# The second layer of a two-layer convolution kernel written as a fixed pipeline over half images

## The chip, the cores and the metric

The kernel runs on one core of one Trainium2 chip. The metric is the device time of one execution, in microseconds (us); lower is better. The core has five engines with instruction queues of their own: TensorE (PE, with its weight loads shown apart as PEld), VectorE (DVE), ScalarE (ACT), GpSimd (POOL) and SyncE (SP). Transfers between DRAM and on-chip memory are issued from the SP and ACT queues and carried out by 16 DMA engines.

## The reference

The input `x` is 32 images of 8 channels and 256 x 256 pixels, float32. Layer 0 normalises it in groups, runs 15 steps of a coupled map lattice beside a small neural convolution, and mixes the two through a gate; the result is added to `x`. Layer 1, the one that the change touches, normalises again, quantises, convolves 3 x 3 over 8 channels and adds its input:

```
def _L1_conv_ref(x, weight, bias):
    sx = 127.0 / jnp.max(jnp.abs(x));  sw = 127.0 / jnp.max(jnp.abs(weight))
    qx = clip(round(x * sx), -127, 127);  qw = clip(round(weight * sw), -127, 127)
    out = conv3x3(qx, qw) / (sx * sw)          # 'same' padding
    return out + bias[None, :, None, None]
x = x + _L0_conv_ref(_gn(x), ...)              # layer 0
x = x + _L1_conv_ref(_gn(x), weight, bias)     # layer 1
```

The scale `sx` needs the largest normalised value of all 32 images, so layer 1 can't start before layer 0 has finished.

## The kernel before

The kernel has two stages. The first (lines 257 to 895) computes layer 0 in groups of four images and leaves each image's result in a DRAM scratch tensor `y_s[b]`. The second stage (lines 898 to 963) reads those tensors and does layer 1; the change is confined to it.

An image lies in the second stage as a tile of 128 partitions by 19 bands by 256 columns. A partition is one of 16 rows times 8 channels, and a band is a set of 16 rows of which 14 are outputs, so that neighbouring bands overlap by two rows. The steps for image `b` are:

- Line 909, `load`: one DMA of 2432 KB brings `y_s[b]` into a `yb` buffer, of which there are four. Images 0 to 2 are loaded from the SP queue, the rest from the ACT queue.
- Line 940: three VectorE instructions subtract the mean and scale, one for the first band, one for bands 1 to 17 (4352 columns) and one for the last band, because the edge bands mask rows. The result is the float32 tile `tq`, of which there is one.
- Line 944: one VectorE instruction over all 4864 columns adds and subtracts 1.5 x 2^23, which rounds to an integer.
- Line 946: one VectorE instruction clips to -127..127 and writes bf16 into `qt`, whose rows are 258 columns long with a zero at either end. There are two `qt`.
- Line 953: for each of ten pairs of bands (the last is a single band) three matmuls of 512 columns add up the three horizontal taps in a PSUM tile, of which there are four. Line 954: ScalarE scales it, adds the bias and writes it to the output tile `ob` (two of them).
- Line 957: one VectorE instruction over 4864 columns adds the image itself, `ob = ob + yb`.
- Line 960: 19 DMAs on the SP queue, one for each band, store the 14 output rows of the 8 channels (112 KB each, the last 32 KB).

In this stage the order of the instructions is a scheduler's: the code gives an order by image, and a planner interleaves images as it expects things to be ready. On VectorE it often lets two line-957 additions or two images' lines 940 to 946 follow each other. On the ACT queue it puts the loads in pairs, after every second image's ten line-954 instructions.

The transfers of all queues share eight completion counters, handed out in turn in the planned order of issue. A transfer waits, on the queue that issues it, until the transfer that had its counter before has landed. In the built program of before nearly every store of line 960 carries such a wait, and when the transfer eight places earlier is an image load, the store waits for the whole load.

Of the kernel before, what the change touches and what calls it, by code (L numbers as in the profile page):

```python
# [31 lines left out]
F32 = mybir.dt.float32  # L32
BF16 = mybir.dt.bfloat16
F32R = mybir.dt.float32r
AF = mybir.ActivationFunctionType
ALU = mybir.AluOpType
AX = mybir.AxisListType
DRAM = bass.MemoryType.DRAM
PSUM = bass.MemoryType.PSUM

P = 128
C = 8
# [4 lines left out]
MAX_Q = 127.0  # L47
ROUND = 1.5 * 2.0**23

NB = 19  # L50
STEP = 14
PW = W + 2
# [61 lines left out]
def kernel(  # L114
# [15 lines left out]
    nc = tc.nc  # L130
    B = x.shape[0]
    V, S, G, T = nc.vector, nc.scalar, nc.gpsimd, nc.tensor

    def dram_ap(t, offset, dims):
        return bass.AP(t.tensor, t.offset + offset, dims)
# [17 lines left out]
    qw = cp.tile([P, 3, P], BF16, name="qw")  # L153
# [6 lines left out]
    mean_y = cp.tile([P, B], F32, name="mean_y")  # L160
# [96 lines left out]
    with ExitStack() as one:  # L257

        one.enter_context(tc.manual_schedule(engines={mybir.EngineType.PE}))
        pool = lambda name, bufs, **kw: one.enter_context(tc.tile_pool(name=name, bufs=bufs, **kw))  # L260
# [115 lines left out]
        def lattice(g):  # L376
# [77 lines left out]
            if g == 0:  # L454
                units[0], dmas = load(0)
                for d in dmas:
                    nc.sync.dma_start(*d)
                for ts in tiles:
                    begin(units[0], ts)
            for c in range(C):  # L460
                u = g * C + c
                ds = units[u]
                for step in range(STEPS):
                    if step == 7 and u + 1 < NG * C:
                        units[u + 1], dmas = load(u + 1)
                        later.extend(dmas)
# [363 lines left out]
        def chain(*gens):  # L830
            for gen in gens:
                yield from gen
# [15 lines left out]
        def both(a, t_a, b, t_b):  # L848

            done_a = done_b = 0.0  # L850
            while a or b:
                if b is None or a and done_a * t_b <= done_b * t_a:
                    w = next(a, None)
                    if w is None:
                        a = None
                        continue
                    done_a += w
                else:
                    w = next(b, None)
                    if w is None:  # L860
                        b = None
                        continue
                    done_b += w
                yield w

        def prep(g, halves):
            return normalise([(b, half) for half in halves for b in range(g * GB, g * GB + GB)])

        def images(f, g):
            for b in range(g * GB, g * GB + GB):  # L870
                yield from f(b)
# [3 lines left out]
        def after(g, gen):  # L875

            while issued[0] < stored[g]:
                yield 4.0
            yield from gen
# [3 lines left out]
        for g in range(NG):  # L883
            fill, t = images(nca, g), T_NCA
            if g:
                fill, t = both(fill, t, after(g - 1, images(gate, g - 1)), T_GATE), t + T_GATE
            if g + 1 < NG:
                fill, t = both(fill, t, prep(g + 1, (0, 1)), T_PREP), t + T_PREP
            if g == 0:
                fill, t = chain(prep(0, (1,)), fill), t + 20.0  # L890
# [7 lines left out]
    with ExitStack() as two:  # L898


        pool = lambda name, bufs, **kw: two.enter_context(
            tc.tile_pool(name=name, bufs=bufs, reuse_waits="tile", **kw)
        )
        tp, qp, op, sp, yp = pool("tp", 1), pool("qp", 2), pool("op", 2), pool("sp", 1), pool("yp", 4)
        ps = pool("ps", 4, space=PSUM)

        def load(b):
            y = yp.tile([P, NB, W], F32, name="yb", tag="yb")
            (nc.sync if b < 3 else nc.scalar).dma_start(
                y, dram_ap(y_s[b], 0, [[W, P], [STEP * C * W, NB], [1, W]])  # L910
            )
            return y

        ys = {b: load(b) for b in range(3)}

        gmax = sp.tile([P, 1], F32, name="gmax")
        V.tensor_reduce(gmax, dev_y, AX.X, ALU.max)
        gall = sp.tile([P, 1], F32, name="gall")
        G.partition_all_reduce(gall, gmax, P, bass.bass_isa.ReduceOp.max)
        sx = sp.tile([P, 1], F32, name="sx")  # L920
        V.reciprocal(sx, gall)
        V.tensor_scalar(sx, sx, MAX_Q, None, ALU.mult)
        inv = sp.tile([P, 1], F32, name="inv")
        V.tensor_tensor(inv, sx, sw, ALU.mult)
        V.reciprocal(inv, inv)
        qs = sp.tile([P, 3, B], F32, name="qs")
        V.tensor_scalar(qs[:, 0, :], rstd_y, sx, None, ALU.mult)
        V.tensor_scalar(qs[:, 1, :], qs[:, 0, :], masks[:, 2:3], None, ALU.mult)
        V.tensor_scalar(qs[:, 2, :], qs[:, 0, :], masks[:, 3:4], None, ALU.mult)
        qt = [qp.tile([P, NB, PW], BF16, name=f"qt{i}", tag=f"qt{i}", bufs=1) for i in range(2)]  # L930
        for t in qt:
            V.memset(t[:, :, 0], 0.0)
            V.memset(t[:, :, PW - 1], 0.0)

        for b in range(B):
            y = ys.pop(b)

            t = tp.tile([P, NB, W], F32, name="tq", tag="tq")
            for k0, k1, i in ((0, 1, 1), (1, NB - 1, 0), (NB - 1, NB, 2)):
                V.tensor_scalar(  # L940
                    t[:, k0:k1, :], y[:, k0:k1, :], mean_y[:, b : b + 1], qs[:, i, b : b + 1],
                    ALU.subtract, ALU.mult,
                )
            V.tensor_scalar(t, t, ROUND, ROUND, ALU.add, ALU.subtract)
            q = qt[b % 2]
            V.tensor_scalar(q[:, :, 1 : 1 + W], t, MAX_Q, -MAX_Q, ALU.min, ALU.max)
            o = op.tile([P, NB, W], F32, name="ob", tag="ob")
            for p in range(10):
                k0, n = 2 * p, (2 if p < 9 else 1)
                pt = ps.tile([P, 512], F32, name="pt2", tag="pt2")  # L950
                pt = pt[:, : n * W].rearrange("p (k w) -> p k w", w=W)
                for dx in range(3):
                    T.matmul(pt, qw[:, dx, :], q[:, k0 : k0 + n, dx : dx + W], start=(dx == 0), stop=(dx == 2))  # L953
                S.activation(o[:, k0 : k0 + n, :], pt, AF.Identity, bias=bv[:, 3:4], scale=inv)  # L954
            if b + 3 < B:
                ys[b + 3] = load(b + 3)
            V.tensor_tensor(o, o, y, ALU.add)
            for k in range(NB):
                rows = STEP if k < NB - 1 else 4
                nc.sync.dma_start(  # L960
                    dram_ap(out, b * C * H * W + STEP * k * W, [[W, rows], [H * W, C], [1, W]]),
                    o[C : C + rows * C, k, :],
                )


# [43 lines left out]
```

## Time and profile before

| | us |
|---|---|
| median of the runs shown (three, 14333.49 to 14348.35) | 14336.46 |
| the profiled execution's own time | 14416.5 |
| its span in the profile | 14414.7 |
| first line-940 instruction of the second stage | 13652.1 |
| second stage from there to the end of the span | 762.6 |
| second stage per image | 23.8 |

| engine | busy over the span |
|---|---|
| PE | 13267.4 us (92%) |
| DVE | 8213.1 us (57%) |
| ACT | 4039.8 us (28%) |
| POOL | 2445.9 us (17%) |

The page puts each engine's busy time beside the span, but these shares are averages over two very different stages. PE is busy at 90% or more in nearly every slice up to the first stage's end; in the last slices it falls to a third. The second stage is read by asking the trace for that stretch alone: the groups of instructions in it, what each engine's and the SP queue's waits ended on, and the chain of work that ended last. "SPq" and "ACTq" are the instruction queues as issuers of DMAs.

### The profile page before, as it was taken

Reading aid. Unit: us, or ns where it says so; the run is one execution under the profiler, and the core shown is the slowest. Engines: PE = TensorE matmul, PEld = TensorE weight load, DVE = VectorE, ACT = ScalarE, POOL = GpSimd, SP = SyncE. Lnnn points to the kernel's source line nnn. Section 1 sums busy time; section 2 is a strip of 40 time slices with the busy share of each in tenths; the row PEclk is TensorE's granted clock in tenths of the full one; section 3 lists DMA queues with packets and bytes.
Section 4 is the critical chain, followed back from the end, with each engine's and each line's share of the span. In section 5 each row is a group of like instructions: output and inputs, shape, how many; then the busy total and the mean of one; then the engine's idle time right before and its main releaser. Section 6 shows DMA issues by size and latency. Waiting matters only on the chain.

```text
span 14414.7 us, 229163 instructions
## 1 busy us (share of the span) xinstructions
PE 13267.4 (92%) x81728; PEld 6423.3 (45%) x81728; DVE 8213.1 (57%) x16290; ACT 4039.8 (28%) x6274; POOL 2445.9 (17%) x4266
## 2 busy tenths in 40 slices
PE   2999999999999999999999999999999999999833
PEld 1554444444444444444444444444444444444311
DVE  3555555555555555555555555555555555555576
ACT  1333232232222222222322223222323222222122
POOL 1111111111111111111111111111111111112300
PEclk9999999999999999999999999999999999999966
DMA  5444444444444444444444434444444433333465
GB/s 148 93 97 92 90 103 106 103 94 100 110 94 100 99 106 94 103 100 95 100 103 107 98 93 106 110 94 94 104 104 98 103 88 88 80 83 78 122 195 176
DMA packets 2259559, 1496.74 MB, mean 104 GB/s; under 512 B 1061248, under 2 KB 2229504, under 8 KB 2258304
## 3 DMA queue, kind: packets, MB, share of 16 engines
q1 hardware_dynamic: 2176976, 1401.95, 41.9%
q10 hardware_dynamic: 81456, 80.12, 1.7%
q8 instruction: 664, 10.88, 0.3%
q14 instruction: 463, 3.79, 0.1%
HBM read 866.48 MB, written 478.69 MB: 93 GB/s over the span
## 4 chain that ended last, share of the span: by engine, by line
PE 70%; DMA 9%; DVE 9%; SPq 5%; issue 3%; POOL 2%; ACT 1%; ACTq 1%; POOLq 0%; DVEq 0%
PE pt L487 31%; PE ph L567 18%; PE pa L759 13%; PE acc L584 7%; DVE gt L495 2%; DMA im<-xp_s 1%; PE pg L725 1%; DMA xp_s<-lo 1%; SPq L545 1%; DVE m_b L500 1%; DMA xb<-in_x_dram 1%; DMA m_a<-m_a 1%; DMA out_dram<-ob 1%; SPq L960 1%; PE pt L953 1%
## 5 line engine op out<-in xcount | busy, mean ns | idle before, releaser
L487 PE MATMUL pt<-m_a,lw 128*64 128x390 f32 x17280 | 5827.0, 497 | 186.4 <-DMA m_a<-m_a 122.4
L487 PE MATMUL pt<-m_b,lw 128*64 128x384 f32 x17280 | 5796.6, 492 | 19.2 <-DVE m_b L410 18.0
L577 ACT ACTIVATE h<-ph,bp_sb 128x512 f32<-128x512 f32 x4096 | 2584.6, 684 | 6491.5 <-PE ph L567 6423.0
L487 PEld LDWEIGHTS pt<-m_a,lw 128*64 128x64 f32 x17280 | 2298.4, 138 | 1884.0 <-issue 1681.2
L487 PEld LDWEIGHTS pt<-m_b,lw 128*64 128x64 f32 x17280 | 2306.6, 138 | 1560.0 <-issue 1423.6
L567 PE MATMUL ph<-im,wp_hi 48*128 48x512 f32 x12288 | 2800.2, 419 | 174.2 <-DVE gt L495 113.1
L567 PE MATMUL ph<-im,wp_lo 48*128 48x512 f32 x12288 | 2675.2, 402 | 0.0
L495 DVE SCALAR_TENSOR_TENSOR gt<-pt,d_b 128x390 f32<-128x390 f32 x2880 | 1605.3, 557 | 1714.7 <-PE pt L487 1711.2
L495 DVE SCALAR_TENSOR_TENSOR gt<-pt,d_a 128x384 f32<-128x384 f32 x2880 | 1580.3, 549 | 1694.5 <-PE pt L487 1694.1
L504 POOL TENSOR_TENSOR m_b<-m_b,junk 128x12 f32<-128x12 f32 x2688 | 795.5, 296 | 8193.8 <-DVE m_b L500 7517.2
L567 PEld LDWEIGHTS ph<-im,wp_hi 48*128 48x128 f32 x12288 | 1417.5, 189 | 1081.7 <-DVE gt L495 303.9
L500 DVE SCALAR_TENSOR_TENSOR m_b<-gt 128x390 f32<-128x390 f32 x2688 | 1546.1, 575 | 44.5 <-DVE gt L495 2.3
L500 DVE SCALAR_TENSOR_TENSOR m_a<-gt 128x384 f32<-128x384 f32 x2688 | 1522.3, 566 | 17.2
L567 PEld LDWEIGHTS ph<-im,wp_lo 48*128 48x128 f32 x12288 | 1417.0, 189 | 217.3
L584 PE MATMUL acc<-h,wu_z 128*32 128x512 f32 x8320 | 1165.6, 603 | 6.1 <-ACT nca L602 5.5
L759 PE MATMUL pa<-xnb,gw 128*64 128x512 f32 (+1 forms) x3840 | 879.9, 588 | 43.7 <-DVE xnb L700 43.5
L759 PE MATMUL pa<-cmb,gw 128*64 128x512 f32 (+1 forms) x3840 | 857.6, 577 | 17.4 <-POOL cmb L681 17.4
L759 PE MATMUL pa<-nb,gw 128*64 128x512 f32 (+1 forms) x3840 | 863.6, 576 | 0.0
L730 POOL TENSOR_TENSOR d<-cmb,nb 128x512 f32<-128x512 f32 x320 | 502.9, 1572 | 1460.6 <-DVE gate L734 1028.5
L700 DVE TENSOR_SCALAR xnb<-xb,sc 128x256 f32<-128x256 f32 x608 | 290.7, 493 | 796.7 <-DMA xb<-in_x_dram 759.5
L953 PE MATMUL pt<-qt,qw 128*128 128x512 bf16 (+1 forms) x960 | 269.5, 451 | 477.0 <-ACT ob L954 425.4
L734 DVE TENSOR_TENSOR gate<-gate,d 128x512 f32<-128x512 f32 x320 | 217.4, 679 | 764.7 <-ACT gate L727 756.7
(132 smaller groups left out, 6928.0 us busy)
## 6 DMA issues: line engine op xcount, KB each, us to landing
im<-xp_s SPq DMA_DIRECT2D x1152, 193.5 KB
im<-xp_s SPq DMA_DIRECT2D x1216, 96.8 KB
d_a<-xq_s SPq DMA_DIRECT2D x2048, 36.0 KB
nb<-nc_s SPq DMA_DIRECT2D x288, 256.0 KB
cq<-cm_s SPq DMA_DIRECT2D x288, 256.0 KB
yb<-y_s ACTq DMA_DIRECT2D x29, 2432.0 KB
xb<-in_x_dram SPq DMA_DIRECT2D x544, 128.0 KB
xp_s<-hi SPq DMA_DIRECT2D x256, 258.0 KB
```

The lines of the kernel that those rows point to most:

```text
L487: T.matmul(pt[half], lw[:, c, k, half], beside if part == 2 else own, start=part < 2, stop=part > 0,)
L495: V.scalar_tensor_tensor(gt, pt, FLOOR, d[:, ts, :], ALU.max, ALU.add)
L500: V.scalar_tensor_tensor(to, gt, 1.0, gt, ALU.subtract, ALU.mult)
L504: G.tensor_tensor(edge, edge, junk.unsqueeze(1).to_broadcast([P, 6, 2]), ALU.mult)
L567: T.matmul(ph[:, :n].rearrange("p (h w) -> p h w", w=W), w[64 * i : 64 * i + 48, dx, :], rhs[:, :, dx : dx + W], start=(dx == 0 and w is w ...
L577: S.activation(h[:, :n], ph[:, :n], AF.Relu, bias=bp_sb)
L584: T.matmul(acc[32 * g : 32 * g + 32, :cols], wu_z[:, 24 - 8 * i : 56 - 8 * i], h, start=first, stop=last,)
L700: V.tensor_scalar(xnb[:, k, 1 : 1 + W], xb[:, k, :], sc[:, i : i + 1], sc[:, 1:2], ALU.subtract, ALU.mult,)
L730: G.tensor_tensor(three(d), cmb[:, :n, 1 : 1 + W], nin, ALU.subtract)
L734: V.tensor_tensor(y[:, :cols], gt[:, :cols], d[:, :cols], ALU.mult)
L759: T.matmul(three[half], gw[:, s * 3 + dx, half], t[:, :n, dx : dx + W], start=(i == 0), stop=(i == 8),)
L953: T.matmul(pt, qw[:, dx, :], q[:, k0 : k0 + n, dx : dx + W], start=(dx == 0), stop=(dx == 2))
```

## The change

Only the second stage changes.

- Its instructions now stand on every engine in the order in which the code gives them; no scheduler moves them.
- An image is worked on in two halves, of bands 0 to 9 and 10 to 18. `tq` and `ob` become half-image tiles (two and four of them), `qt` becomes two half tiles for each of two images, and there are eight PSUM tiles. The 3 x 3 taps need no other half's data, since bands overlap.
- Rounding and clipping are arranged anew on VectorE. One instruction adds the rounding constant and takes the maximum with the constant minus 127; a second takes the minimum with the constant plus 127, subtracts the constant and writes bf16.
- In each iteration VectorE first scales and quantises both halves of image `b`, then adds both halves of image `b - 1`. SP stores bands 0 to 12 of image `b - 1`. ScalarE evacuates image `b`, then its queue stores bands 13 to 18 of image `b - 1` and issues the load of image `b + 3`.
- The first four images are loaded from SP. The zero columns of `qt` are set by GpSimd, not VectorE.

In the order of the built program the counters of the stores and loads are handed out, from the fifth image on, so: store 1 of SP for image j, store 1 of ACT for image j - 1, and so on in turn up to the sixth of each; then store 7 of SP, the load that stands behind the ACT stores of image j - 1, and stores 8 to 13 of SP. That makes 20 transfers an image, and each waits for the one eight places before it in that list. ACT's first store of an image so waits for the load of the iteration before, and ACT's fourth for SP's store 13 of the same image.

```diff
+        two.enter_context(tc.manual_schedule())
...
-        tp, qp, op, sp, yp = pool("tp", 1), pool("qp", 2), pool("op", 2), pool("sp", 1), pool("yp", 4)
-        ps = pool("ps", 4, space=PSUM)
+        tp, qp, op, sp, yp = pool("tp", 2), pool("qp", 1), pool("op", 4), pool("sp", 1), pool("yp", 4)
+        ps = pool("ps", 8, space=PSUM)
...
-            (nc.sync if b < 3 else nc.scalar).dma_start(
+            (nc.sync if b < 4 else nc.scalar).dma_start(
...
-            V.tensor_scalar(t, t, ROUND, ROUND, ALU.add, ALU.subtract)
-            q = qt[b % 2]
-            V.tensor_scalar(q[:, :, 1 : 1 + W], t, MAX_Q, -MAX_Q, ALU.min, ALU.max)
...
+        HALVES = ((0, 10), (10, NB))
+        def scaled(b, y, h):
+            h0, h1 = HALVES[h]
+            t = tp.tile([P, 10, W], F32, name="tq", tag="tq")
             for k0, k1, i in ((0, 1, 1), (1, NB - 1, 0), (NB - 1, NB, 2)):
+                k0, k1 = max(k0, h0), min(k1, h1)
+                if k0 < k1:
+                    V.tensor_scalar(
+                        t[:, k0 - h0 : k1 - h0, :], y[:, k0:k1, :], mean_y[:, b : b + 1],
+                        qs[:, i, b : b + 1], ALU.subtract, ALU.mult,
+                    )
+            t = t[:, : h1 - h0, :]
+            V.tensor_scalar(t, t, ROUND, ROUND - MAX_Q, ALU.add, ALU.max)
+            return t
+        def quantised(b, t, h):
+            V.tensor_scalar(qt[b % 2][h][:, :, 1 : 1 + W], t, ROUND + MAX_Q, ROUND, ALU.min, ALU.subtract)
...
+        last = None
+        for b in range(B + 1):
+            if b < B:
+                y = ys[b]
+                ts = [scaled(b, y, h) for h in range(2)]
+                for h in range(2):
+                    quantised(b, ts[h], h)
+            if last:
+                i, os_ = last
+                yi = ys.pop(i)
+                for h, (h0, h1) in enumerate(HALVES):
+                    o = os_[h][:, : h1 - h0, :]
+                    V.tensor_tensor(o, o, yi[:, h0:h1, :], ALU.add)
+                store(nc.sync, i, os_[0], 0, range(0, 10))
+                store(nc.sync, i, os_[1], 1, range(10, 13))
+            done = last
+            if b < B:
+                last = b, [convolved(b, h) for h in range(2)]
+            if done:
+                i, os_ = done
+                store(nc.scalar, i, os_[1], 1, range(13, NB))
+                if i + 4 < B:
+                    ys[i + 4] = load(i + 4)
```

`convolved(b, h)` holds the matmuls and the ScalarE instruction of before for the bands of one half, and `store` the DMA of before for the bands that it is given.

More of the change, by code (lines that the diff above doesn't have):

```diff
@@ L912, in load @@
             return y
-        ys = {b: load(b) for b in range(3)}
+        ys = {b: load(b) for b in range(4)}
         gmax = sp.tile([P, 1], F32, name="gmax")
@@ L929, with convolved @@
         V.tensor_scalar(qs[:, 2, :], qs[:, 0, :], masks[:, 3:4], None, ALU.mult)
[L930 to L938, printed above, removed]
-            for k0, k1, i in ((0, 1, 1), (1, NB - 1, 0), (NB - 1, NB, 2)):
[L940 to L944, printed above, removed]
-            q = qt[b % 2]
[L946 to L949, printed above, removed]
+        qt = [[qp.tile([P, n, PW], BF16, name=f"qt{i}{j}") for j, n in enumerate((10, 9))] for i in range(2)]
+        for t in (*qt[0], *qt[1]):
+            G.memset(t[:, :, 0], 0.0)
+            G.memset(t[:, :, PW - 1], 0.0)
+        HALVES = ((0, 10), (10, NB))
+        def scaled(b, y, h):
+            h0, h1 = HALVES[h]
+            t = tp.tile([P, 10, W], F32, name="tq", tag="tq")
+            for k0, k1, i in ((0, 1, 1), (1, NB - 1, 0), (NB - 1, NB, 2)):
+                k0, k1 = max(k0, h0), min(k1, h1)
[9 more added lines that the diff above has]
+            V.tensor_scalar(qt[b % 2][h][:, :, 1 : 1 + W], t, ROUND + MAX_Q, ROUND, ALU.min, ALU.subtract)
+        def convolved(b, h):
+            h0, h1 = HALVES[h]
+            o = op.tile([P, 10, W], F32, name="ob", tag="ob")
+            for k0 in range(0, h1 - h0, 2):
+                n = min(2, h1 - h0 - k0)
                 pt = ps.tile([P, 512], F32, name="pt2", tag="pt2")
@@ L952, with store @@
                 for dx in range(3):
-                    T.matmul(pt, qw[:, dx, :], q[:, k0 : k0 + n, dx : dx + W], start=(dx == 0), stop=(dx == 2))
+                    T.matmul(
+                        pt, qw[:, dx, :], qt[b % 2][h][:, k0 : k0 + n, dx : dx + W],
+                        start=(dx == 0), stop=(dx == 2),
+                    )
                 S.activation(o[:, k0 : k0 + n, :], pt, AF.Identity, bias=bv[:, 3:4], scale=inv)
[L955 to L958, printed above, removed]
+            return o
+        def store(queue, b, o, h, ks):
+            for k in ks:
                 rows = STEP if k < NB - 1 else 4
-                nc.sync.dma_start(
+                queue.dma_start(
                     dram_ap(out, b * C * H * W + STEP * k * W, [[W, rows], [H * W, C], [1, W]]),
-                    o[C : C + rows * C, k, :],
+                    o[C : C + rows * C, k - HALVES[h][0], :],
                 )
+        last = None
[21 more added lines that the diff above has]
+                    ys[i + 4] = load(i + 4)
 def kernel(
```

## The prediction

> **What bounds the kernel now.** The first stage keeps its instructions and their order on every engine, so only the second stage counts. I asked for the busy time of the engines in stretches of it (columns: stretch, length, busy time and count of each engine, PE clock, DMA share, GB/s).
>
> ```profile
> 13650.00:13666.00 16.00, 2.69 (x7) 0.99 (x7) 14.78 (x14) 0.78 (x1) 0.38 (x1) 0.50 1.10 348
> 14000.00:14100.00 100.00, 35.83 (x130) 14.58 (x129) 69.37 (x25) 27.90 (x42) 0.00 (x0) 0.66 0.62 190
> ```
>
> The first row is the loading of the first images, the second the steady state. There no engine is full: DVE 69%, PE 36%, ACT 28%, DMA 62%. Next, the groups of instructions from 13660 on, shapes apart:
>
> ```profile
> L954 ACT ACTIVATE ob<-pt,bv,inv 128x512 f32<-128x512 f32 x288 | 204.3, 777 | 536.7 <-DMA out_dram<-ob 456.9 <-PE pt L953 52.4 <-DMA yb<-y_s 22.8
> L946 DVE TENSOR_SCALAR qt<-tq 128x4864 bf16<-128x4864 f32 x32 | 167.1, 5221 | 122.7 <-PE pt L953 121.0
> L957 DVE TENSOR_TENSOR ob<-ob,yb 128x4864 f32<-128x4864 f32 x32 | 167.1, 5221 | 96.0 <-ACT ob L954 77.1 <-DMA out_dram<-ob 18.9
> L944 DVE TENSOR_SCALAR tq<-tq 128x4864 f32<-128x4864 f32 x31 | 83.5, 2694 | 1.1
> L940 DVE TENSOR_SCALAR tq<-yb,mean_y,qs 128x4352 f32<-128x4352 f32 x31 | 78.8, 2541 | 0.0
> L940 DVE TENSOR_SCALAR tq<-yb,mean_y,qs 128x256 f32<-128x256 f32 x62 | 25.3, 408 | 0.7
> ```
>
> ScalarE stood 457 us for stores to release `ob`; VectorE's own waits follow from that (through PE and ACT). So the stores: their issue times, what SP waited for, and the chain of one pair of images.
>
> ```profile
> L960 SPq DMA_DIRECT2D out_dram<-ob x608: 652/817/1345, 13682.5 to 14411.6; - x152
> L909 ACTq DMA_DIRECT2D yb<-y_s x29: 366/366/395, 13637.5 to 14315.2; - x29
> ```
> ```profile
> SPq L960 <- DMA yb<-y_s: 125.8, 26, 12.0
> SPq L960 <- DVE ob L957: 49.0, 12, 4.6
> ```
> ```profile
> 14013.93 10.31 DMA yb<-y_s
> 14024.24 0.02 issue
> 14024.25 0.83 SPq L960
> ...
> 14028.75 6.96 DMA out_dram<-ob
> 14035.71 0.02 issue
> ...
> 14035.77 4.37 DMA out_dram<-ob
> 14040.15 0.78 ACT ob L954
> ```
>
> Stores stand on SP every 0.89 us (14024.25, then 14026.04 and 14027.82, each two further). 608 x 0.89 = 541 us, plus about 190 us of waits, fills the 732 us from the first store to the end. The largest wait, 126 us, is a store whose counter was last held by an image load. The bound is the SP queue: 19 stores (16.9 us) and some 6 us of waits make the 23.8 us an image.
>
> **What the Trainium skill says.** "DMA: Bandwidth & Descriptors", section "Issuing engines are not separate DMA queues": transfers from all issuers share the same 16 DMA engines, and a second issuer saves only sequencer time. Here that time is the bound (0.89 us a store at 62% DMA share), so the trace agrees there is something to save. "VectorE: DVE Perf Modes", section "What auto-detection actually checks": an instruction with one source runs two columns a cycle if source and destination are in on-chip memory with outermost dimensions both even or equal. The trace agrees: line 944 takes 0.55 ns a column, line 946, whose destination is 19 rows at a pitch of 258, takes 1.07, and this line, whose destination is rows at a pitch of 258 in even number, 0.67 with its fixed part:
>
> ```profile
> L342 DVE CAST hi<-xr 128x1024 fp32r<-128x1024 f32 x128 | 88.4, 690 | 264.8 <-DMA xp_s<-hi 195.2 <-DMA im<-xp_s 34.0 <-issue 22.3
> ```
>
> **The change, part by part, for one image.**
>
> *VectorE.* Lines 940's two shapes give 0.521 ns a column plus 0.275 us. Scaling: two edge bands 0.82, 2304 columns 1.48, 2048 columns 1.34, sum 3.63. Rounding with the lower clip, in place as line 944 (0.521 ns plus 0.16): 2560 and 2304 columns, 1.49 + 1.36 = 2.85. Upper clip into `qt`: ten rows are even, so I take 1.49; nine rows against a flat source of 2304 stay at one column a cycle, 2304 x 1.042 + 0.15 = 2.55; sum 4.04 (bounds: 2.85 if both are fast, 5.37 if neither). Addition at line 957's rate: 2.82 + 2.55 = 5.37. Total 15.9, with ten gaps of some 0.03 us 16.2; before it was 16.5. So VectorE gains next to nothing, and 32 x 16.2 is its floor.
>
> *PE and ACT.* Work is unchanged: 279.3 / 32 = 8.7 and 222.4 / 32 = 6.95 us. Eight PSUM tiles let PE run eight pairs ahead of ScalarE. VectorE adds an image one iteration after quantising it, so ACT may be late by about 12 us before VectorE stands.
>
> *SP.* 13 x 0.89 = 11.5 us instead of 16.9. *ACT queue.* 6.95 + 6 stores + one load of 0.37. No store of this shape was issued from ACT before. The nearest rows (load 0.366 there against 0.386 on SP) say the queues cost the same, so 0.89, 5.3 us in all; bounds 0.31 (the first stage's small zero stores on ACT) and 1.8 (both queues served by one generator).
>
> *DMA.* 4.59 MB an image. Loads alone ran at 348 GB/s, mixtures at up to 386: 12 to 13 us an image, not the bound.
>
> *The new wait.* ACT's first store waits until the load issued one iteration earlier has landed. Behind it on ACT's queue are five stores, the next load, and then the ten evacuations of the next image, for which PSUM, the additions and SP's stores wait. So loads form a ring: landing time L, then six stores (5.3), then the next load. L: the load at 14013.93 took 10.31 us with some 4.5 stores beside it (the bytes moved up to 14026 less its own 2.49 MB); the one at 13682.54 took 12.23 with about 10. So L = 8.8 + 0.34 k. With SP storing every 0.89 us, about six of its 13 stores fall into the six-store stretch of ACT, k is 7 to 9 and L 11.2 to 11.9. Ring: 11.6 + 5.4 = 17.0, and I allow 0.2 for a counter not yet free: 17.2 us an image. That is above VectorE's 16.2, so the ring binds. Other waits on counters (ACT's fourth store on SP's 13th; SP's ninth on ACT's fourth) close rings of 13 us or less and hide under it.
>
> *Start.* VectorE starts at 13652.1 as before, held by the reduction over partitions. The eight small sets on GpSimd end before the first matmul. Iteration 0 takes 10.7, iteration 1 starts at 13662.8. Load 4 leaves after SP's first 13 stores, at 13690; loads 5, 6 and 7 follow at spacings of 17 to 20 us, since here the counters go round in another order, and load 7 goes at about 13746.
>
> *Sum.* Load 31 is 24 rounds later: 13746 + 24 x 17.2 = 14159, landing at 14170.5. Then image 31 is scaled and quantised (10.7), image 30's first half added (2.8), and from there SP has 26 stores (23.1) and a landing of 2.9: 39.5 us. End 14210, against 14414.7: a gain of 205 us. The profiled execution (14416.5) is 80 us above the median of the runs shown; the second stage being a twentieth of it, I take the gain as it is: 14336.5 - 205 = **14131**.
>
> **Rivals.**
>
> *VectorE binds.* If ACT's stores are cheaper, or fewer SP stores meet the loads, the ring falls below 16.2. Image 31 starts at 13662.8 + 30 x 16.2 = 14149; with 39.5 the end is 14188, or 14110 as a time (14085 if both upper clips are fast). Against it: the ring is longer by the numbers above. If neither half clips fast, VectorE needs 17.5, and the time is 14150.
>
> *The two queues pay for each other.* Their stores may share what takes the 0.82 us. Six stores of ACT then take about 10 us, the ring is 21.8 us, the end 110 us later: 14245; half of it gives 14190. For it: one shared set of DMA engines, and stores that landed in 2.1 us alone took 6.96 beside a load. Against it: SP went on storing at its cadence when ACT issued a load.
>
> *Slower.* The same ring, at the price of 25.7 us a round: the point from which the gain is gone, since 205 / 24 = 8.5 more. With L = 12 each of ACT's stores would have to hold its queue for 2.3 us. Against it: the longest issue of a store on SP was 1.345. If it is 3 us, the ring is 30 us and the time 14435.
>
> *The change doesn't do what it says*: the half of nine rows keeps the old clip rate, so the new clip is fast in one half only. That is in the sum already.
>
> **Chances.** Ring at about 17.2: 0.5, its own range 14105 to 14160. VectorE binds: 0.2. Queues pay for each other: 0.22. A ring near or above 24 us: 0.08, of which 0.05 end as a loss, 0.02 within 0.2% and 0.01 as a small gain. Range 14080 to 14215: it leaves out the dearer half of the third case and the last. A measurement of this kernel can tell about 0.2% (29 us) from no change. Faster 0.93, same 0.02, slower 0.05.
>
> **What the new profile would show.** Stores on SP and ACT at 0.8 us each; second stage near 558 us; PE as before. The ring is right if ACT's first store of each image waits for `yb`, at one load each 17 us. If VectorE binds, its share is above 95% and its idle time nil. If queues pay for each other, issue times rise above 1.2 us. The clip into ten rows should take 1.5 us, into nine 2.55. The prediction fails if the landing of loads grows with both queues storing, or if the wait for the counter is placed differently from the built order.

## The result and the profile after

| | before | after |
|---|---|---|
| median of four runs each, us | 14337.08 (14333.49 to 14348.35) | 14132.78 (14127.72 to 14143.41) |
| ratio to before, 95% interval | | 0.9857 (0.984 to 0.9874) |
| the profiled execution's own time, us | 14416.5 | 14143.41 |
| its span, us | 14414.7 | 14141.6 |
| first scaling instruction of the second stage | 13652.1 | 13591.7 |
| second stage from there to the end of the span | 762.6 | 549.9 |

The change saves 204 us by the medians. The spans differ by more, 273 us, because the profiled execution of before was 60 us longer in the first stage, whose instructions are the same in both. The second stage alone is 213 us shorter, from 23.8 to 17.2 us an image, and that is the figure to work with.

The busy time of a stretch in the steady state of the kernel after (columns as in the prediction: stretch, length, PE, PEld, DVE, ACT, POOL, PE clock, DMA share, GB/s):

```profile
13800.00:13900.00 100.00, 51.57 (x180) 21.06 (x180) 90.92 (x60) 39.57 (x60) 0.00 (x0) 0.70 0.86 274
```

VectorE has gone from 69% to 91% and the DMA engines from 0.62 to 0.86. Neither is full. The groups of instructions of the kernel after from 13600 on, shapes apart, say what the rest of VectorE's time is:

```profile
L967 ACT ACTIVATE ob<-pt,bv,inv 128x512 f32<-128x512 f32 x288 | 197.0, 792 | 340.2 <-DMA out_dram<-ob 292.6 <-PE pt L963 34.1 <-DVE tq L944 13.5
L992 DVE TENSOR_TENSOR ob<-ob,yb 128x2560 f32<-128x2560 f32 x32 | 90.1, 2816 | 1.7 <-ACT ob L967 1.7
L953 DVE TENSOR_SCALAR qt<-tq 128x2304 bf16<-128x2304 f32 x32 | 81.6, 2549 | 0.0
L953 DVE TENSOR_SCALAR qt<-tq 128x2560 bf16<-128x2560 f32 x31 | 46.2, 1489 | 0.0
L944 DVE TENSOR_SCALAR tq<-yb,mean_y,qs 128x256 f32<-128x256 f32 x62 | 25.4, 409 | 40.2 <-DMA yb<-y_s 40.2
```

VectorE's only stop worth a name is the last row's: 40 us, before the first band of an image, for the image's load. Before the change it stood 121 us for PE at line 946 and 96 us at line 957. The clip (line 953) takes 1.49 us into ten rows and 2.55 us into nine. ScalarE still shows 293 us of idle time, but VectorE no longer waits for ScalarE (1.7 us), so that idle time costs nothing now.

Which of them sets the pace is read from the chain of work that ended last, here one round of the steady state up to the load that begins the next (columns: start, us, what):

```profile
13853.42 11.35 DMA yb<-y_s
...
13864.85 0.83 ACTq L973
...
13868.40 0.82 ACTq L973
...
13869.32 0.68 ACTq L973
13870.00 0.04 issue
13870.04 11.40 DMA yb<-y_s
```

Between the two loads lie six stores of the ACT queue (line 973), and nothing else is in the chain: a load lands, the store that waits for its counter goes, five more follow it, the next load goes. Such a closed chain, each round of which must end before the next can begin, is called a ring here. The rounds next to this one take 16.6 to 17.3 us. The issues of the kernel after, by line and queue (columns: count, shortest, median and longest ns, first and last start):

```profile
L973 SPq DMA_DIRECT2D out_dram<-ob x416: 807/813/1282, 13614.7 to 14138.2; - x139
L973 ACTq DMA_DIRECT2D out_dram<-ob x192: 666/823/1243, 13617.1 to 14133.4; - x192
L910 ACTq DMA_DIRECT2D yb<-y_s x28: 373/460/466, 13623.8 to 14091.2; - x28
```

A store costs the same on both queues, 0.81 and 0.82 us. Load 7 went at 13679.50 and load 31, the last, at 14091.2: 24 rounds of 17.15 us, in which a load took 11.2 to 13.1 us to land, 11.8 on average. And SP's own waits for a load have nearly gone, from 126 us in 26 waits to:

```profile
SPq L973 <- DMA yb<-y_s: 13.0, 3, 6.6
```

### The profile page after: what moved, and what is told of

The parts are those of the page before. It is cut to its first block, busy times and chain, and to the rows that moved or that the text cites. A ratio compares the mean times of both kernels' runs of the same rounds, so it can differ in the third digit from the quotient of the medians.

```text
span 14141.6 us, 229388 instructions
## 1 busy us (share of the span) xinstructions
PE 13255.7 (94%) x81728; PEld 6412.2 (45%) x81728; DVE 8184.6 (58%) x16414; ACT 4036.5 (29%) x6274; POOL 2452.2 (17%) x4274
## 4 chain that ended last, share of the span: by engine, by line
PE 73%; DMA 9%; DVE 8%; SPq 4%; issue 3%; ACTq 1%; POOL 1%; ACT 1%; POOLq 0%; DVEq 0%
PE pt L487 32%; PE ph L567 19%; PE pa L759 14%; PE acc L584 7%; DVE gt L495 2%; DMA yb<-y_s 2%; PE pg L725 1%; DMA im<-xp_s 1%; SPq L545 1%; DMA xp_s<-lo 1%; DVE m_b L500 1%; DMA xb<-in_x_dram 1%; DMA m_a<-m_a 1%; ACTq L973 1%; SPq L444 1%
## 5 line engine op out<-in xcount | busy, mean ns | idle before, releaser
L500 DVE SCALAR_TENSOR_TENSOR m_a<-gt 128x384 f32<-128x384 f32 x2688 | 1528.2, 569 | 17.2
L759 PE MATMUL pa<-cmb,gw 128*64 128x512 f32 (+1 forms) x3840 | 858.5, 577 | 17.3 <-POOL cmb L681 17.3
L700 DVE TENSOR_SCALAR xnb<-xb,sc 128x256 f32<-128x256 f32 x608 | 292.0, 495 | 762.6 <-DMA xb<-in_x_dram 725.9
L771 ACT ACTIVATE r<-pa,bv 128x512 f32<-128x512 f32 x320 | 213.0, 666 | 1538.6 <-PE pa L759 1538.5
```

Source lines behind the costliest of these rows:

```text
L500: V.scalar_tensor_tensor(to, gt, 1.0, gt, ALU.subtract, ALU.mult)
L700: V.tensor_scalar(xnb[:, k, 1 : 1 + W], xb[:, k, :], sc[:, i : i + 1], sc[:, 1:2], ALU.subtract, ALU.mult,)
L759: T.matmul(three[half], gw[:, s * 3 + dx, half], t[:, :n, dx : dx + W], start=(i == 0), stop=(i == 8),)
L771: S.activation(r1[:, : n * W], pa[:, : n * W], AF.Relu, bias=bv[:, 0:1])
```

## The experiments

When the experiments ran, the kernel before took 14382 to 14386 us (medians of seven to nine runs), some 45 us more than above. So each run is compared by its ratio to the runs of before beside it, and by the length of its second stage in its trace, which is 549.9 us for the kernel after. The kernel after itself was run once more there:

> The changed kernel itself, for comparison on one chip with the two below. All theories: a ratio of 0.986 to the kernel before, second stage 550.

It took 14162.8 us, 219 us less than before there, ratio 0.9849 (0.9835 to 0.9862), second stage 551.6 us. The two kernels whose stage was measured twice differ by 1.7 and 1.4 us in it, so stage lengths, each from one trace, can be compared to about 2 us. Mean rounds below are taken from load 7 to load 31, as above.

| run | second stage, us | time, us | ratio to before, 95% interval |
|---|---|---|---|
| kernel after, again | 551.6 | 14162.8 | 0.9849 (0.9835 to 0.9862) |
| nine-row clip fast | 554.8 | 14186.09 | 0.9858 (0.9842 to 0.9875) |
| loads from GpSimd | 534.0 | 14151.32 | 0.9839 (0.9825 to 0.9854) |
| both of these | 537.1 | 14145.14 | 0.9828 (0.9813 to 0.9842) |
| four stores on ACT | 581.9 | 14200.34 | 0.9871 (0.9856 to 0.9886) |
| nine stores on ACT | 530.9 | 14156.99 | 0.9839 (0.9824 to 0.9853) |
| the same, again | 532.3 | 14145.08 | 0.9839 (0.9826 to 0.9852) |
| nine stores on ACT, nine-row clip fast | 529.8 | 14158.58 | 0.9841 (0.9828 to 0.9855) |
| load ahead of ACT's stores | 630.1 | 14247.59 | 0.9906 (0.9891 to 0.9921) |
| all stores on SP | 618.8 | 14241.86 | 0.9898 (0.9882 to 0.9915) |
| kernel before, six stores on ACT | 704.7 | 14321.34 | 0.9951 (0.9936 to 0.9966) |

The theory is that the ring of loads and ACT stores binds. The first rival is that VectorE does.

**Is it VectorE?** The nine-row half's `tq` gets rows of 258 columns, so that its clip reads and writes rows of one pitch.

```diff
-            t = tp.tile([P, 10, W], F32, name="tq", tag="tq")
+            t = tp.tile([P, 10, W + 2 * h], F32, name="tq", tag=f"tq{h}", bufs=1)[:, :, :W]
```

> The changed kernel, with the second half's tq tile at a row pitch of 258, so that the upper clip reads nine rows and writes nine rows. Its 2.55 us should fall to about 1.36, so VectorE has about 1.2 us less to do for each image; nothing else changes. Ring theory: VectorE only waits longer for loads, period 17.15 as before, second stage 548 to 550, time about 14132. VectorE theory: 32 x 1.2 = 38 us less, about 14095.

The nine-row clip fell from 2.55 to 1.49 us, which leaves VectorE some 0.9 us an image less work (the rounding, now on the same padded rows, rose from 1.36 to 1.49). The second stage took 554.8 us, no less than before the edit (the 3 to 5 us more are about what its loads took longer to land, 11.94 us on average against 11.77). What VectorE saved it waits: its stops at line 992 rose from 2 to 18 us, and its waits for the load, in the kernel with the fast nine-row clip, rose from 40.2 us in 24 waits to

```profile
DVE tq L944 <- DMA yb<-y_s: 55.6, 26, 3.7
```

and its busy time in the steady state fell:

```profile
13934.90:14034.90 100.00, 50.05 (x180) 20.85 (x179) 84.21 (x58) 38.37 (x59) 0.00 (x0) 0.70 0.84 270
```

An engine with less work and the same end isn't the bound. This rival falls.

**Cutting the ring.** If the ring binds, a load that doesn't stand behind ACT's stores should free it. Loads 4 to 31 go out from GpSimd, whose transfers don't take part in the counters of the other two queues in the built program; in the trace of this kernel no store waits for a load.

```diff
-            (nc.sync if b < 4 else nc.scalar).dma_start(
+            (nc.sync if b < 4 else nc.gpsimd).dma_start(
```

> The changed kernel, with loads 4 to 31 issued from GpSimd's queue instead of ACT's. They then use completion counters of their own, and no store waits for a load. Ring theory (load landing plus six ACT stores sets 17.15 us an image): the ring is cut, VectorE's 15.3 us an image binds, second stage 550 - 24 x 1.85 = about 505 us, time about 14090. VectorE theory (the 17.15 us are VectorE's work and the gaps between its instructions): no change, 550 us and 14133. DMA theory (the 16 DMA engines at a share of 0.86 are what limits): no change either, or slower if loads from GpSimd's queue are made less efficiently.

The second stage fell to 534.0 us: the ring was the bound, since cutting it moved the end and relieving VectorE didn't. But the gain was 16 to 18 us instead of 45. A stretch of this kernel says what bound next:

```profile
13807.10:13907.10 100.00, 56.06 (x186) 21.25 (x185) 96.68 (x62) 39.67 (x60) 13.44 (x6) 0.73 0.84 275
```

VectorE is at 97%, so it now binds, but in most rounds with a period of 15.97 us (the loads at 13808.69 and 13824.66), where its instructions need 15.3: so far apart start images 1 to 3 in the kernel after, before the ring holds them. The groups of the same kernel show the difference in one place:

```profile
L949 DVE TENSOR_SCALAR tq<-tq 128x2560 f32<-128x2560 f32 x32 | 67.5, 2110 | 1.1
L949 DVE TENSOR_SCALAR tq<-tq 128x2304 f32<-128x2304 f32 x32 | 43.5, 1360 | 1.1
```

The rounding of the ten-row half takes 2.11 us on average instead of 1.49, that of the nine-row half the 1.36 that it took before. The timeline of one image:

```profile
13808.69 2.24 POOL L910 DMA_DIRECT2D yb<-y_s  x1 [13.73 <-DVE ob L992]
13810.02 2.20 DVE L949 TENSOR_SCALAR tq<-tq 128x2560 f32<-128x2560 f32 x1
```

GpSimd takes 2.24 us to issue a load, released by the addition that frees the image buffer, and so always at the same place in VectorE's order. The slowed instruction is the one that overlaps the end of the issue. The first two and the last two images, which no load of GpSimd meets, show 1.49 us. The Trainium skill, "SBUF — State Buffer", section "Who interferes with whom", names a cause that my 505 us left out: VectorE, when it takes two columns a cycle, and GpSimd, which needs the same port to write a transfer's descriptors, lock each other out for a whole instruction. This trace agrees as far as it goes: line 944's 2304 columns, already running when the issue begins, keep their 1.47 us, and the next instruction pays; it ends 1.29 us after the issue, a little less than its own 1.49. 28 slowed instructions at 2.20 and four at 1.49 make the 67.5 us of the row. So 0.71 us of each image, 20 of the missing 29 us, are this collision. Another 7 us are stops of VectorE at line 992, where ScalarE was late because stores had not yet freed `ob`.

With both edits together VectorE is relieved as well:

> Loads from GpSimd's queue and the fast clip in both halves together. In the run with loads from GpSimd's queue VectorE was the bound (16.0 us an image, 0.6 of it one rounding instruction made slower while GpSimd issued a load). If VectorE still binds, the period falls by 1.2 to about 14.8, second stage about 495. If stores and their counters bind right behind it, the period stays near 16 and the stage near 530. DMA theory: 0.86 x 17.15 = 14.7 us of transfers an image is the floor, so not below 480.

The stage didn't get shorter (537.1 us). VectorE is back at 91%, and what it was relieved of it now waits before the second addition of an image, where it stood 7.0 us with loads from GpSimd alone. The stretch and this row in the kernel with both edits:

```profile
13813.60:13913.60 100.00, 58.83 (x183) 21.74 (x182) 90.72 (x61) 39.76 (x60) 13.45 (x6) 0.70 0.86 279
```
```profile
L992 DVE TENSOR_TENSOR ob<-ob,yb 128x2304 f32<-128x2304 f32 x32 | 81.7, 2554 | 39.8 <-ACT ob L967 23.0 <-DMA out_dram<-ob 16.8
```

Most rounds of this kernel take 15.03 us, which is what VectorE needs with the collision and without the slow clip (15.3 + 0.7 - 0.9). But every second or third takes 16.4 to 21.4 us, because `ob` comes late: stores have not yet freed it. In the chain near the end of the stage single stores take 8.9 to 9.2 us to land. SP waited as long for counters held by other stores when VectorE was the bound (131.0 us, here 133.9), so that wait alone says nothing. So with ring and VectorE out of the way, the stores themselves hold the mean round at 16.5 us. Whether it is their counters or what they share with the loads on the DMA engines, no run separates.

**Is it the number of ACT stores, or the counters?** Two stores are moved from ACT to SP.

```diff
-                store(nc.sync, i, os_[1], 1, range(10, 13))
+                store(nc.sync, i, os_[1], 1, range(10, 15))
-                store(nc.scalar, i, os_[1], 1, range(13, NB))
+                store(nc.scalar, i, os_[1], 1, range(15, NB))
```

> The changed kernel, with four instead of six stores of an image on ACT's queue and fifteen on SP's. Counting the stores on ACT's queue alone, the ring is 11.7 + 4 x 0.87 = 15.2 and VectorE binds at 15.3: about 14090. Through the counters, the load's counter goes to SP's thirteenth store, ACT's fourth store waits for SP's fifteenth and the load stands behind it: 11.7 + 3 x 0.89 + landing 2.5 + 0.9 + 0.4 = about 18, second stage about 570, time about 14153. VectorE and DMA theories: no change.

The stage took 581.9 us. With two ACT stores fewer (1.7 us) each round became 0.9 us longer, 18.1 us, as the counters say and the count doesn't. That makes 22 us of the 32; 9 more stand between the last load and the end of the stage, 59 us instead of 50, and the expected 570 us left them out. The chain of this kernel shows the new ring, which now runs over SP:

```profile
13858.92 12.65 DMA yb<-y_s
...
13871.64 0.81 SPq L973
...
13872.50 0.82 SPq L973
...
13873.42 2.45 DMA out_dram<-ob
...
13875.95 0.67 ACTq L973
...
13876.65 12.06 DMA yb<-y_s
```

The load's counter now passes to a store on SP. The last ACT store before the next load waits until the second store after that one has landed (2.45 us), and the load lands in 12.7 us on average.

In the other direction, ACT stores the whole second half, nine bands (`range(10, 10)` on SP, which is none, and `range(10, NB)` on ACT):

> The changed kernel with nine stores on ACT's queue and ten on SP's. Counting ACT's stores, the ring is 11.7 + 9 x 0.87 + 0.4 = 19.9 us, second stage about 620. Through the counters ACT's fourth store is the one that waits for the load, and six stores and the load come after it: 11.5 + 6 x 0.87 + 0.4 = 17.1, second stage about 550, as in the changed kernel.

Its chain:

```profile
13809.14 10.43 DMA yb<-y_s
...
13819.59 0.82 ACTq L973
...
13824.06 0.68 ACTq L973
13824.74 0.04 issue
13824.78 10.34 DMA yb<-y_s
```

Again six stores after the load, though nine are on the queue: the first three go before the store that waits. But the load lands in 10.4 us here and 10.9 on average, instead of 11.8, so the round is 15.6 us here and 16.1 on average. The stage is 530.9 us, shorter than expected. That the load lands earlier because SP issues only ten stores beside it goes the way of the prediction's L = 8.8 + 0.34 k; it was not varied by itself. A repeat:

> Nine stores of an image on ACT's queue, ten on SP's, as before. Ring theory: the load meets ten SP stores instead of thirteen and lands in 10.4 us, ring 15.6, VectorE 15.3 right under it: second stage 531, about 19 us less than the changed kernel. A theory in which only the number of ACT's stores counts would have it slower.

gave 532.3 us and the same ratio, 0.9839 (0.9826 to 0.9852). In stage length this beats the kernel after by 19 us both times. In time the gain is 0.1%, and the intervals overlap. The DMA engines' share rose to 0.90 with it, so the 0.86 of the kernel after wasn't their limit: the rival that they bind falls too. VectorE is near its limit there (94.65 us busy in 100). So the clip was tried once more, where it might count:

> Nine stores on ACT's queue and the fast clip in both halves. Ring theory: VectorE's 1.2 us an image come off a VectorE that nearly binds, so the period falls from about 15.8 to the ring's 15.6 and no further; second stage about 525. If VectorE bound there, it would fall by 38 us to about 493.

529.8 us: nothing gained. VectorE again waits for loads instead (32.0 us, without the fast clip 19.8), so with nine stores the ring still sets the pace, a little above VectorE.

**The place of the load.** The load is put ahead of ACT's six stores of the same iteration.

```diff
+                if i + 4 < B:
+                    ys[i + 4] = load(i + 4)
                 store(nc.scalar, i, os_[1], 1, range(13, NB))
-                if i + 4 < B:
-                    ys[i + 4] = load(i + 4)
```

> The changed kernel, with the load put ahead of the six ACT stores in the code. If only the order on ACT's queue made the ring, the load no longer stands behind the stores: period near VectorE's 15.3, time about 14090. If the counters make it, a new ring takes its place, since the load now hands its counter to SP's ninth store, and the next load waits for SP's thirteenth: landing 11.7, five SP stores 4.4, landing of a store 2.5, together about 18.6 us an image, second stage about 585 us, time about 14165. VectorE and DMA theories: no change, 550 us.

630.1 us, 20.2 us a round: slower, as the ring theory foretold, but by more, and not by the way that it foretold. No load is in the chain of this kernel:

```profile
13852.90 2.59 DMA out_dram<-ob
...
13856.15 2.79 ACT ob L967 x4
...
13858.97 2.84 DVE ob L992
...
13861.82 0.81 SPq L973
...
13866.26 4.92 DMA out_dram<-ob
...
13871.25 0.83 ACTq L973
...
13873.96 2.55 DMA out_dram<-ob
```

The new ring goes through the output tiles: a store lands and frees `ob`, ScalarE fills the tile, VectorE adds, SP issues five stores, an ACT store waits 4.9 us for the sixth to land, three ACT stores later the fourth must land before ScalarE can go on. The four `ob` tiles did not set the pace before this edit and do after it. Moving one transfer in the order passes its counter to another store, and that sets up a ring that is not read from the moved transfer alone.

**Which part of the change brought the gain?** One run keeps halves, order and clip, and puts all 19 stores on SP (`range(10, NB)` there; ACT's line is left out):

> The changed kernel with all 19 stores of an image on SP, one part of the change undone. SP then issues 19 x 0.89 = 16.9 us an image. By the counters SP's last store of an image waits for a load, and the next load for SP's fourth store of the next image: about 1.6 us more, 18.5 us an image, second stage about 615, time some 65 us above the changed kernel's. If the queue were not what bound the kernel before, and halves and order made the gain, the second stage would stay at 550.

618.8 us, as expected. SP's waits for ScalarE and for loads are now these, none longer than 1.1 and 2.3 us; its waits for other stores reach 1.5 us, and one of 18.8 us stands at the start:

```profile
SPq L973 <- ACT ob L967: 63.3, 116, 1.1
SPq L973 <- DMA yb<-y_s: 25.6, 28, 2.3
```

SP's issuing, 608 x 0.89 = 541 us, now fills nine tenths of the 593 us from its first store to its last. So halves, fixed order and clip, with the waits that go with them, bring 144 of the 213 us, and the second queue the other 69; which of the three brings how much no run separates. The other run keeps the kernel before, whole images and scheduler, and moves only the last six stores of each image to ACT:

```diff
-                nc.sync.dma_start(
+                (nc.sync if k < 13 else nc.scalar).dma_start(
```

> The kernel before with one thing changed: stores of bands 13 to 18 on ACT's queue; whole images, the scheduler's order and two ob tiles stay. If the SP queue is the bound, as the prediction has it, most of the gain comes from this alone: 11.5 us of issue on SP, second stage about 620 instead of 763. If halves and a fixed order are needed, since evacuations wait for all stores of the image two before, most of it stays: 700 or more.

704.7 us: 58 us gained, a little over a quarter. (With the 144 us of the other part that makes 202 of the 213.) The order isn't quite that of before, as the scheduler planned anew: every second load now stands directly behind an image's ACT stores, and most of an image's scaling comes between two additions. So the 58 us are those of the second queue together with the order that the scheduler then chose. SP is no longer the bound, and nearly a third of the stage it waits for sums:

```profile
SPq L960 <- DVE ob L957: 220.1, 17, 15.6
SPq L960 <- DMA yb<-y_s: 71.4, 14, 5.6
```

Its chain, over one pair of images, is a ring of its own:

```profile
13870.83 13.04 DMA yb<-y_s
...
13883.89 0.83 SPq L960
...
13890.16 2.51 DMA out_dram<-ob
13892.67 2.30 ACT ob L954 x4
13894.97 9.69 DMA yb<-y_s
13904.67 5.22 DVE ob L957
...
13915.19 12.87 DMA yb<-y_s
```

A load lands, a store that had to wait for it and seven more go out on SP, the last lands and frees `ob`, ScalarE works, and then another load has to come in before the addition, after which ACT's stores lead to the next load: 44.4 us for two images, of which two loads in series are 22.7. Pieces of this ring (a load, some stores, a store's landing, an evacuation) stand in the chain of the kernel before that the prediction showed.

## Why the prediction was right, and where it wasn't

Predicted 14131, measured 14132.8, a gain of 205 against 204 us. The ring that the forecast rests on is in the trace and of the right size. That the two gains agree to 1 us is luck: the stage alone became 213 us shorter, and a second comparison of the same two kernels gave 219 us. Step by step:

- *The new wait, ring of 17.2 us.* Right in mechanism and size: 17.15 us a round, with L of 11.8 on average, single loads 11.2 to 13.1 (predicted 11.2 to 11.9), and six stores in 5.2 to 5.5 (5.3). Cutting the ring shortened the stage; the fast clip did not. That the predicted chain is the one in the trace is shown. L's dependence on the stores beside it is only consistent with three kernels (means of 10.9 us with ten SP stores an image, 11.8 with 13, 12.7 with 15).
- *ACT queue, 0.89 us a store.* Right: 0.82 us of issue plus 0.04 to 0.1 to the next, as on SP. With that the rival that the two queues pay for each other falls; it would have shown over 1.2 us.
- *VectorE, 15.9 us of instructions.* Each duration came out as computed: clip 1.49 and 2.55, additions 2.82 and 2.55. The step "ten gaps of some 0.03 us" was wrong in sign. The durations sum to 15.89 us, but VectorE's busy time is 90.92 / 6 = 15.2 us an image (60 instructions, six images, in 100 us): consecutive instructions overlap in the trace. The floor was about 15.3 us (the distance of images 1 to 3 in the kernel after, and 15.97 less the 0.71 of the collision in the run with loads from GpSimd), not 16.2, so the ring stood nearly 2 us above VectorE and not 1.
- *Start and end.* Load 7 went 87.8 us after the stage's start, not 94. The spacings from load 4 to load 7 were as forecast (18.7, 17.0 and 20.0 us), but load 4 went after 32.1 us, not 38: the forecast had it leave behind SP's 13 stores, and it left behind ACT's own six, which began at 13617.13, 2.5 us after SP's first. From load 31 to the end it took 50.4 us, not 51.0. With 24 x 0.05 us for the ring, this makes the stage 550 us instead of 558. These 8 us don't show in the medians: the four runs of each kernel spread by 15 to 16 us, and the profiled execution of before, whose stage of 762.6 us the forecast was set against, isn't one of them.
- *What bounds the kernel now: "the bound is the SP queue".* This step doesn't hold as it stands. SP's own issuing, 541 us, is 74% of the 732 us from its first store on, and the chain of before that the prediction shows in part goes on so:

```profile
14047.69 0.39 SPq L960
...
14052.63 2.10 DMA out_dram<-ob
...
14055.81 4.01 PE pt L953 x9
...
14061.48 10.60 DMA yb<-y_s
```

From load to load that is a ring of 47.55 us for two images, 23.8 an image, which is the measured pace. Only 9.4 us of it are SP issuing stores; in six stretches of 100 us from 13700 to 14300 it is 12 to 23% of the chain. The landing of one load takes 10.3, the landings of three stores 13.4, and ScalarE and TensorE in between 14.3. So what the prediction read as waits of 6 us beside the queue's own time was the larger part of a ring. Freeing SP of six stores brought 58 us where the scheduler and the whole-image tiles stayed; with all stores still on SP, the change's order and halves took 144 us away (618.8 us), and only there does SP's issuing nearly fill the time. With SP relieved in a scheduler's order a ring remained too, in which the landings of two loads are 22.7 of 44.4 us and the issue of stores 11.6. The number came out right because the forecast subtracted nothing from the waits of before: it built the time of the new order from the new order's own waits.
- *Sums.* The 16.9 and 6 us of that step make 22.9, not 23.8; the rest are the 30 us before the first store. For the rival with the dearer queues, 14131 and 110 us make 14241, not 14245. Neither bears on the forecast.

The rival "slower" had as its price 2.3 us an ACT store; the longest was 1.24. Three experiments missed in size. With loads from GpSimd (534 us instead of 505) the collision and the late `ob` were left out. With nine stores on ACT (531 instead of 550) the six stores after the load were foreseen, and the load's landing was taken as that of the kernel after. With the load ahead of the stores (630 instead of 585) the counter was followed, and the wait for `ob` that joined in was not.

## What to carry to other kernels

Where transfers share completion counters in turn, write down for each transfer which earlier one it waits for, on which queue, and what stands behind it there; then add up each closed ring: the longest one set the period here. Before calling a queue the bound, because its issues and waits fill its time, add up its issuing along one round of the chain (here 9.4 of 47.6 us), and ask what its waits close, since they may belong to a ring that a second queue doesn't open (here it brought 58 of 213 us). And when relieving one resource, know the next floors: here ring, VectorE and stores lay at 17.2, 15.3 and 16.5 us, so that no single further edit brought more than 4% of the stage.

## What the runs showed of the hardware

- Issuing a 2432 KB load from GpSimd takes 2.24 us, from ACT 0.37 to 0.47, and the VectorE instruction that starts during the issue (rounding, 2560 columns float32) takes 2.20 us instead of 1.49. All 28 of these instructions that coincided with the end of an issue were slowed, and the other four were not. The coincidence is shown; the port lock as its cause is the skill's, and no run here put the issue beside an instruction of one column a cycle to test it.
- Consecutive VectorE instructions overlap in the records: ten instructions with durations summing to 15.9 us take 15.2 to 15.3 us.
- Stores of 112 KB cost 0.81 to 0.83 us of the issuing queue's time on SP and ACT alike, also when both issue at once.
- The same nine-row clip costs 2.55 us from a flat source and 1.49 us from a source with the destination's row pitch. This is what the Trainium skill, "VectorE: DVE Perf Modes", section "What auto-detection actually checks", lets one expect: nine is odd, so the rate hangs on source and destination having the same outermost dimension, and a flat source has lost its rows.
